# The first block of an FP4 feed-forward stage: a third pair of accumulators, products in fixed turn, an earlier table load, other PSUM banks

## The chip, the cores and the metric

The kernel runs on one core of a Trainium2 chip. The metric is the device time of one launch in microseconds. The engines named are TensorE (PE, its weight loads PEld), VectorE (DVE), ScalarE (ACT), GpSimd (POOL) and SyncE (SP, which here issues transfers).

## The reference

Two transformer layers run on 2 sequences of 1024 tokens with 512 channels. The change lies in the feed-forward part of the first layer, whose weights are stored as 4-bit numbers with a scale for every 128 inputs:

```python
def _L0_ffn_ref(x, gate_up_packed, gate_up_scales, down_packed, down_scales):
    I = gate_up_packed.shape[0] // 2                      # 1408
    w_gu = _dequant_fp4(gate_up_packed, gate_up_scales, 128)
    w_down = _dequant_fp4(down_packed, down_scales, 128)
    gate_up = einsum('bsh,oh->bso', x, w_gu)
    gate, up = gate_up[..., :I], gate_up[..., I:]
    h = silu(gate) * up
    y = einsum('bsi,hi->bsh', h, w_down)
    return y / sqrt(mean(y * y, -1) + 1e-6)

x = layernorm(x + L0_attn(x))      # stage 1 of the kernel
x = layernorm(x + L0_ffn(x))       # stage 2, the FP4 stage
x = layernorm(x + L1_attn(x))      # gated linear attention
x = layernorm(x + L1_ffn(x))       # routed feed-forward, top 512 of 1024 tokens
```

## The kernel before

The 2048 tokens are cut into four blocks of 512 (`NB = 4`), and the 512 channels into four slices of 128 (`KC = 4`), which are also the groups that share a scale. The 1408 hidden units are eleven tiles of 128 (`NI = 11`), numbered by `f`.

**Stage 1** is the linear attention of the first layer. For its last tiles it turns the queries (`transposed`, L197), multiplies them with a matrix (`project`, L217, tile `ao`), adds the result to the row of x on VectorE (L383) and takes statistics. Exponentials run on ScalarE (L270), and the queries are weighed on VectorE with a small tile `z` of two buffers (L355 to L360). At its end the FP4 scales are turned and copied (L399 to L403). The first block of x is split into a high and a low part, `x1Th` and `x1Tl`, which together stand for float32 in a faster format; their product with the unpacked weights `wgu` is two matmuls.

**Stage 2** runs over the blocks, and in each block over f. For one f, `scaled_sums` makes eight groups of two matmuls: for each of the four slices k a group for gate and one for up. A group fills one PSUM bank. For k = 0 ScalarE copies the bank, times its scale, into an accumulator (L470). For other k VectorE multiplies and adds into it (L476). For some f (`by_three`: odd f and f from 8 on in block 0) the last group of up goes another way: ScalarE copies it (L473) and GpSimd adds it (L474). Then ScalarE applies silu to gate (L660), and GpSimd multiplies with up into h (L661).

Accumulators are two "rooms" each for gate and up, taken in turn: f can begin to accumulate when h of f - 2 is made. PSUM has eight banks, given out in rings. Stage 2 splits them into a ring of six for gate and up (and the transposes) and a ring of two for the down products (L631). The bank of a group is fixed in the order of the program, so each group waits until the group six places before it has been read.

The order in which an engine gets its instructions comes from a scheduler, which follows the order of the program but may move an instruction that seems ready before others. `tc.issue_after(ins)` keeps all instructions of a `with` that are on the engine of `ins` behind `ins`. In the kernel before, the matmuls of each f stand behind the last one of the f before (L658); inside an f the groups are free. In f = 8 and 9 a function `quarter` puts in four transposes after k = 1 and after k = 3, which prepare the next block (`split_quarter`, L208 to L212).

In block 0, GpSimd also normalises the fourth block of x, a quarter after each of f = 0, 2, 4 and 6 (`norm_tiles`, L564 to L573, with one power L570). From the second block on, the down products of the block before (`down`, matmuls L512 and L521, tile `P`) follow the gate and up products of f = 1, 4 and 7; they use seven products of half size in place of eight, for which GpSimd makes sums of h (`S`, L527) and, in block 1, of the weights (`T1`, `T2`, `T4`, L457).

Of the kernel before, what the change touches and what calls it, by code (L numbers as in the profile page):

```python
# [10 lines left out]
F32 = mybir.dt.float32  # L11
# [4 lines left out]
AF = mybir.ActivationFunctionType  # L16
# [5 lines left out]
P = 128  # L22
# [4 lines left out]
NI = I_FF // P  # L27
# [46 lines left out]
def body(ctx: ExitStack, tc: tile.TileContext, a: dict, out: bass.AP):  # L74
    nc = tc.nc
# [5 lines left out]
    sp = ctx.enter_context(tc.tile_pool(name="small", bufs=3))  # L81
# [4 lines left out]
    rings, turn_of = {"mm": range(4), "acc": range(4, 8)}, {"mm": 0, "acc": 0}  # L86
# [6 lines left out]
    def mm_bank(name):  # L93
        return bank("mm", name)

    def acc_bank(name):
        return bank("acc", name)
# [4 lines left out]
    def const(name):  # L102
        at, n = _AT[name]
        return table[:, at : at + n]

    ident = const("ident")

    def place_w(i, name):
        return wpool.tile([P, KC, C], F32, tag=f"A{i}", name=name)
# [6 lines left out]
    def load_w(dst, name):  # L116
        nc.sync.dma_start(out=dst, in_=a[name].rearrange("(k p) o -> p k o", p=P))
# [73 lines left out]
    last_turned = [None]  # L191

    def transposed(x, name):

        pt = mm_bank(name)
        for k in range(KC):
            ins = nc.tensor.transpose(pt[:, k * P : (k + 1) * P], x[:, k * P : (k + 1) * P], ident).ins  # L197
        last_turned[0] = ins
        return pt

    def split_tiles(blk):

        i, j = ((1, 1), (2, 0), (0, 2), (1, 1))[blk]
        hi = xT_slot(i, "x1Th", F32R)
        lo = wpool.tile([P, KC, 512], F32R, tag=f"A{j}", name="x1Tl")
        return hi, lo

    def split_quarter(parts, blk, i):  # L208
        hi, lo = (t[:, :, i * P : (i + 1) * P] for t in parts)
        pt = transposed(x_t[blk][:, i], "x1Tp").rearrange("p (k t) -> p k t", k=KC)  # L210
        nc.scalar.copy(hi, pt)
        nc.vector.tensor_sub(lo, pt, hi.bitcast(F32))  # L212
# [9 lines left out]
    wgu = wfp4.tile([P, KC, 2 * I_FF], F32R, name="wgu")  # L222
# [56 lines left out]
    for b in range(B):  # L279
        acc = [acc_bank(f"xk{b}_{c}") for c in range(KC)]  # L280
# [18 lines left out]
        if b == 0:  # L299
            first = [mm_bank("kp") for _ in range(4)]  # L300
# [68 lines left out]
        for n in range(10):  # L369
# [5 lines left out]
            if n >= 1 and n <= 8:  # L375
                i = n - 1
                blk = 2 * b + i // 4
# [4 lines left out]
                x = x_t[blk][:, i % 4]  # L382
# [9 lines left out]
            if b == 1 and n in (2, 3, 4, 5):  # L392
                if n == 2:
                    parts = split_tiles(0)
# [6 lines left out]
    pg = mm_bank("pg")  # L401
    nc.tensor.transpose(pg[:, : KC * FG], sg, ident[: KC * FG, : KC * FG])
    nc.scalar.copy(scale, pg[:, : KC * FG])  # L403
    s1.close()


# [8 lines left out]
    def xT_tile(name):  # L415
        return xT_slot(next(free), name)

    def turn(blk, part=range(4)):

        if 0 in part:  # L420
            xT[blk] = xT_tile("x2T")
        for i in part:
            pt = transposed(x_t[blk][:, i], "x2Tp")
            nc.scalar.copy(xT[blk][:, :, i * P : (i + 1) * P], pt.rearrange("p (k t) -> p k t", k=KC))
        return last_turned[0]
# [14 lines left out]

    with tc.tile_pool(name="s2", bufs=1) as wk2:
        NP = (NI - 1) // 2
        rooms = {n: [wk2.tile([P, 512], F32, name=f"{n}{i}") for i in range(2)] for n in ("gate", "up")}
        spare, junk = b2, rw
        extra = [wk2.tile([P, 3, 512], F32, name="h_even")]
        T1, T2, T4 = (wk2.tile([P, NP, 256], F32, name=f"T{i}") for i in (1, 2, 4))
        S = wk2.tile([P, NP, 2, P], F32, name="S")
        extra.append(wk2.tile([P, 3, 512], F32, name="h_odd"))


# [3 lines left out]
        def sums_of_wdn():  # L454
            for dst, x, y in ((T1, B12, B11), (T2, B22, T1), (T4, B21, T2), (B12, B22, B12)):
                for j in (slice(0, 3), slice(3, NP)):
                    yield nc.gpsimd.tensor_sub(dst[:, j], x[:, j], y[:, j])  # L457

        def scaled_sums(f, parts, gate, up, by_three, beside=None):

            for k in range(KC):
                for acc, at, name in ((gate, f, "gatep"), (up, NI + f, "upp")):
                    ps = mm_bank(name)
                    for x in parts:
                        ins = nc.tensor.matmul(  # L465
                            ps, wgu[:, k, at * P : (at + 1) * P], x[:, k], start=x is parts[0], stop=x is parts[1]
                        ).ins
                    s = scale[:, k * FG + at : k * FG + at + 1]
                    if k == 0:
                        nc.scalar.activation(acc, ps, AF.Copy, scale=s)  # L470
                    elif k == KC - 1 and acc is up and by_three:
                        third = (spare, junk)[f % 2]
                        nc.scalar.activation(third, ps, AF.Copy, scale=s)  # L473
                        nc.gpsimd.tensor_add(acc, acc, third)  # L474
                    else:
                        last = nc.vector.scalar_tensor_tensor(acc, ps, s, acc, ALU.mult, ALU.add).ins  # L476
                if beside is not None:
                    beside(k)
            return ins, last

        class Hidden:
# [15 lines left out]

        of_S = lambda j: S[:, j]
        last_p = [None]
# [59 lines left out]
        def take(pieces, n):  # L559
            for _ in range(n):  # L560
                next(pieces, None)
# [66 lines left out]
                    yield  # L628
                layernorm(x_t[self.blk], self.mv)

        rings["mm"], rings["acc"] = (0, 1, 2, 3, 6, 7), (4, 5)  # L631
        wsums = sums_of_wdn()
        now, pieces = None, iter(())
        for blk in range(NB):
            h = Hidden(blk)
            for f in range(NI):
                if f == 0 and blk:
                    with tc.issue_after(hm):
                        take(pieces, 1)
                gate, up = (rooms[n][(blk * NI + f) % 2] for n in ("gate", "up"))  # L640
                if f == 8:

                    if blk < NB - 1:
                        coming = split_tiles(blk + 1)
                    else:
                        Wig = place_w(0, "Wig")
                        load_w(Wig, "WigT")

                def quarter(k):
                    if k % 2 and f in (8, 9):  # L650
                        i = 2 * (f - 8) + k // 2
                        if blk < NB - 1:
                            split_quarter(coming, blk + 1, i)
                        else:
                            turn(0, (i,))

                by_three = f % 2 == 1 or f >= 8 if blk == 0 else f >= 8 and blk < NB - 1
                with tc.issue_after(mm) if blk or f else ExitStack():  # L658
                    mm, st = scaled_sums(f, parts, gate, up, by_three, quarter)
                sl = nc.scalar.activation(gate, gate, AF.Silu).ins  # L660
                hm = nc.gpsimd.tensor_mul(h.chunk(f), up, gate).ins  # L661
                with tc.issue_after(mm), tc.issue_after(st), tc.issue_after(hm), tc.issue_after(sl):
                    if blk == 0 and f in (0, 2, 4, 6):
                        norm_tiles(3, late, (f // 2,))
                    for _ in range((1, 5, 1, 1)[f] if blk == 1 and f < 4 else 0):
                        next(wsums)
                    if blk > 1 and f in old_steps:
                        old_steps[f]()

                    if blk and f in (1, 4, 7):  # L670
                        take(pieces, {1: 22, 4: 32, 7: 24}[f])
                        mm = last_p[0]
                    if blk == NB - 1 and f == 9:
                        now.squares(range(4))
                        now.power()
            parts = coming
            old, now = now, Normed(blk)
            pieces = down(h, now.room)
            if blk > 0:
                old_steps = old.steps()  # L680
# [52 lines left out]
    T1, T2, T4 = gsums[1][:, 1], gsums[2][:, 0], gsums[2][:, 1]  # L733
# [44 lines left out]
    def scores(blk, gates, beside=None):  # L778
# [51 lines left out]
        for i in range(4):  # L830
# [4 lines left out]
            nc.tensor.matmul(up, gates.kd[:, t].rearrange("p r d -> p (r d)"), x_t[blk][:, i], start=True, stop=True)  # L835
            S = wk.tile([P, C], F32, tag="S", name="S", bufs=4)
            if t == 0:
                ins = nc.vector.tensor_copy(S, up).ins
            else:
                ins = nc.vector.scalar_tensor_tensor(  # L840
                    S, state[blk // 2, t], decay[:, i : i + 1], up, ALU.mult, ALU.add
                ).ins
            state[blk // 2, t + 1] = S
        return ins

    def attend(blk):
# [4 lines left out]
        for c in range(KC):  # L851
            op = mm_bank("op")
            cut = slice(c * P, (c + 1) * P)
            for i in range(4):
                S = state.get((blk // 2, 4 * (blk % 2) + i))
                oi = op[:, i * P : (i + 1) * P]
# [557 lines left out]
```

## Time and profile before

| what | us |
|---|---|
| median of 3 runs | 1013.36 (1012.85 to 1015.86) |
| profiled execution, its own time | 1015.42 |
| its span, first to last instruction | 1013.6 |
| TensorE busy | 990.1 (98%) |
| VectorE busy | 645.6 (64%) |
| GpSimd busy | 299.5 (30%) |
| ScalarE busy | 276.1 (27%) |
| first unhoisted gate product of block 0 | at 253.65 |
| first down product (block 1, after f = 1) | at 313.83 |
| end of the FP4 stage's last product (about) | at 552.8 |

Times inside the span are counted from its first instruction. A busy time says how long an engine worked and not whether anything waited for it; whether a wait matters is read from the timeline of the engine that sets the pace in that stretch.

### The profile page before, as it was taken

How to read it: one execution, taken by the hardware profiler on the slowest of the kernel's cores; microseconds unless marked ns; L12 is line 12 of the kernel's file. 1: busy time of each engine (PE TensorE's matmuls, PEld its weight loads, DVE VectorE, ACT ScalarE, POOL GpSimd, SP SyncE). 2: the span in 40 equal slices, each digit the busy share in tenths (PEclk: the TensorE clock that was granted, in tenths of full speed). 3: DMA queues.
4: the chain of work that ended last, by engine and by line, in shares of the span. 5: the costliest groups of instructions: out<-in, count | busy, mean ns of one | idle time of the engine just before them, and what ended most of it. 6: DMA issues, size and time to landing. Idle time of an engine off the chain costs nothing.

```text
span 1013.6 us, 10955 instructions
## 1 busy us (share of the span) xinstructions
PE 990.1 (98%) x4061; PEld 709.1 (70%) x4061; DVE 645.6 (64%) x1233; ACT 276.1 (27%) x465; POOL 299.5 (30%) x277
## 2 busy tenths in 40 slices
PE   8999999999899999999999999999999999999996
PEld 3454444544668888888888854687777688888885
DVE  1246754476786576676666258556698795789744
ACT  2223232232453235235233143142130124220000
POOL 1100351004567626566556103201014003000022
PEclk9999999999999999999999999999999999999999
DMA  9611113110000000000011140000003412140011
GB/s 345 199 52 57 43 58 113 32 32 0 1 1 0 1 1 1 1 1 11 1 42 42 40 179 0 1 1 0 1 7 108 126 52 84 42 167 1 0 42 42
DMA packets 25688, 48.81 MB, mean 48 GB/s; under 512 B 4652, under 2 KB 6316, under 8 KB 25123
## 3 DMA queue, kind: packets, MB, share of 16 engines
q1 hardware_dynamic: 22995, 42.85, 12.8%
q0 software_dynamic: 1920, 4.22, 1.1%
q10 hardware_dynamic: 720, 1.05, 0.3%
q8 instruction: 32, 0.52, 0.2%
q14 instruction: 21, 0.17, 0.1%
HBM read 39.70 MB, written 10.52 MB: 50 GB/s over the span
## 4 chain that ended last, share of the span: by engine, by line
PE 83%; issue 8%; DVE 4%; ACT 2%; POOL 2%; DMA 0%; POOLq 0%; ACTq 0%; DVEq 0%
PE P L512 12%; PE yp L1158 9%; PE hp L1079 9%; PE gatep L465 8%; PE upp L465 8%; PE qp L217 5%; PE xk L286 5%; PE ao L217 5%; PE kp L217 4%; PE ao L962 3%; PE go L918 2%; PE kp L303 1%; PE lp L432 1%; PE P L521 1%; PE up L835 1%
## 5 line engine op out<-in xcount | busy, mean ns | idle before, releaser
L181 POOL TENSOR_TENSOR rs<-rs,table 128x4 f32<-128x4 f32 (+1 forms) x21 | 19.6, 937 | 324.4 <-DVE rs L180 324.1
L476 DVE SCALAR_TENSOR_TENSOR gate<-gatep,scale,gate 128x512 f32<-128x512 f32 x132 | 98.1, 743 | 13.9 <-PE gatep L465 8.7
L476 DVE SCALAR_TENSOR_TENSOR up<-upp,scale,up 128x512 f32<-128x512 f32 x119 | 88.4, 743 | 2.5 <-PE upp L465 1.5
L465 PE MATMUL gatep<-x1Th,wgu 128*128 128x512 f32 x176 | 73.7, 428 | 4.0 <-ACT gate L470 3.5
L465 PE MATMUL upp<-x1Th,wgu 128*128 128x512 f32 x176 | 70.0, 402 | 0.4 <-ACT gate L470 0.4
L465 PE MATMUL upp<-x1Tl,wgu 128*128 128x512 f32 x176 | 69.1, 396 | 0.0
L465 PE MATMUL gatep<-x1Tl,wgu 128*128 128x512 f32 x176 | 68.5, 398 | 0.0
L661 POOL TENSOR_TENSOR h<-up,gate 128x512 f32<-128x512 f32 x32 | 41.1, 1285 | 85.7 <-ACT gate L660 80.6
L470 ACT ACTIVATE gate<-gatep,scale 128x512 f32<-128x512 f32 x44 | 30.3, 689 | 123.7 <-PE gatep L465 106.7
L512 PE MATMUL P<-wdn,h 128*128 128x256 f32 x256 | 60.5, 379 | 0.0
L217 PE MATMUL qp<-Wq,x0T 128*128 128x512 f32 x128 | 57.6, 592 | 0.0
L217 PE MATMUL ao<-G,qT 128*128 128x512 f32 x128 | 57.5, 595 | 0.0
L286 PE MATMUL xk<-k,x 128*128 128x512 f32 x128 | 56.7, 592 | 0.0
L962 PE MATMUL ao<-W1o,uT 128*128 128x512 f32 x128 | 55.6, 592 | 0.0
L512 PEld LDWEIGHTS P<-wdn,h 128*128 128x128 f32 x256 | 48.5, 190 | 6.8
L866 POOL TENSOR_TENSOR sum<-sum,sq 128x512 f32<-128x512 f32 x12 | 18.2, 1518 | 107.6 <-issue 83.7
L286 PEld LDWEIGHTS xk<-k,x 128*128 128x128 f32 x128 | 24.3, 190 | 30.6 <-issue 29.9
L217 PEld LDWEIGHTS ao<-G,qT 128*128 128x128 f32 x128 | 24.1, 190 | 30.2 <-issue 28.9
L271 DVE SCALAR_TENSOR_TENSOR k<-kp,e 128x512 f32<-128x512 f32 x16 | 11.0, 691 | 53.7 <-ACT e L270 48.2
L465 PEld LDWEIGHTS gatep<-x1Th,wgu 128*128 128x128 f32 x176 | 32.9, 190 | 16.9 <-ACT gate L470 9.6
L962 PEld LDWEIGHTS ao<-W1o,uT 128*128 128x128 f32 x128 | 24.0, 190 | 28.7 <-issue 27.7
L217 PE MATMUL kp<-Wk,x0T 128*128 128x512 f32 x96 | 43.4, 593 | 0.2 <-DVE k L271 0.2
(338 smaller groups left out, 2125.7 us busy)
## 6 DMA issues: line engine op xcount, KB each, us to landing
pk<-in_gu SPq DMA_DIRECT2D x16, 352.0 KB, 3.8
x<-in_x SPq DMA_DIRECT2D x4, 1024.0 KB, 12.8
w<-in_w SPq DMA_DIRECT2D x1, 4096.0 KB, 14.7
xs<-picked SPq DMA_DIRECT2D x4, 1024.0 KB, 5.1
out<-x SPq DMA_DIRECT2D x4, 1024.0 KB, 4.5
w<-in_w SPq DMA_DIRECT2D x4, 1024.0 KB, 6.6
x0T<-in_xT SPq DMA_DIRECT2D x3, 1024.0 KB, 8.8
pk<-in_dn SPq DMA_DIRECT2D x11, 256.0 KB, 3.5
```

The source lines that it names most:

```text
L181: power = nc.gpsimd.tensor_tensor(rs[:, :n], rs[:, :n], const("mhalf")[:, :n], ALU.pow).ins
L217: nc.tensor.matmul(ps, lhs[:, k], w[:, k], start=start and k == 0, stop=stop and k == KC - 1)
L286: nc.tensor.matmul(acc[c], x_t[2 * b + i // 4][:, i % 4, c * P : (c + 1) * P], k, start=i == 0, stop=i == 7)
L465: ins = nc.tensor.matmul(ps, wgu[:, k, at * P : (at + 1) * P], x[:, k], start=x is parts[0], stop=x is parts[1]).ins
L470: nc.scalar.activation(acc, ps, AF.Copy, scale=s)
L476: last = nc.vector.scalar_tensor_tensor(acc, ps, s, acc, ALU.mult, ALU.add).ins
L512: last_p[0] = nc.tensor.matmul(cut, x(j)[:, r], w[:, j], start=j == 0, stop=j == NP - 1 and tail is None).ins
L661: hm = nc.gpsimd.tensor_mul(h.chunk(f), up, gate).ins
L918: nc.tensor.matmul(ps[:, 256 * m : 256 * m + 256], w[:, k, m], b[:, k, 256 * half : 256 * half + 256], start=k == 0, stop=k == KC - 1,)
L962: nc.tensor.matmul(ao[i], uT[blk][:, k, i * P : (i + 1) * P], W1o[:, k], start=n == 0, stop=n == 3)
L1079: nc.tensor.matmul(ps[:, 256 * j : 256 * j + 256], w[:, k, 2 * g + j], x[:, k], start=k == 0, stop=k == 1)
L1158: nc.tensor.matmul(ps[:, 256 * r : 256 * r + 256], x(r, j), w(j), start=j == 0, stop=j == NJ - 1)
```

## The change

Four things change. Block 0 has three rooms for gate and up, the third lying in the tile `T4`, which is not written until block 1; later blocks keep two. Inside an f each group of matmuls stands behind the group before it in program order, and so do the transposes of `quarter`. A one-column silu at the end of stage 1, which writes a `z` buffer that nothing reads, puts silu's table load there. The down products get the two banks that stage 1's last accumulations used, here 6 and 7, and gate and up get the other six.

```diff
+    nc.scalar.activation(sp.tile([P, 16], F32, tag="z", name="first", bufs=2)[:, :1], ident[:, :1], AF.Silu)
     s1.close()
...
-        rooms = {n: [wk2.tile([P, 512], F32, name=f"{n}{i}") for i in range(2)] for n in ("gate", "up")}
+        rooms = [[wk2.tile([P, 512], F32, name=f"{n}{i}") for n in ("gate", "up")] for i in range(2)]
...
         S = wk2.tile([P, NP, 2, P], F32, name="S")
+
+        rooms.append([T4.rearrange("p j c -> p (j c)")[:, i * 512 : (i + 1) * 512] for i in range(2)])
...
         def scaled_sums(f, parts, gate, up, by_three, beside=None):
+            ins = None
             for k in range(KC):
                 for acc, at, name in ((gate, f, "gatep"), (up, NI + f, "upp")):
                     ps = mm_bank(name)
-                    for x in parts:
-                        ins = nc.tensor.matmul(
-                            ps, wgu[:, k, at * P : (at + 1) * P], x[:, k], start=x is parts[0], stop=x is parts[1]
-                        ).ins
+                    with ExitStack() if ins is None else tc.issue_after(ins):
+                        for x in parts:
+                            ins = nc.tensor.matmul(
+                                ps, wgu[:, k, at * P : (at + 1) * P], x[:, k], start=x is parts[0], stop=x is parts[1]
+                            ).ins
...
-                if beside is not None:
-                    beside(k)
+                with tc.issue_after(ins):
+                    ins = beside(k) or ins
             return ins, last
...
-        rings["mm"], rings["acc"] = (0, 1, 2, 3, 6, 7), (4, 5)
+        rings["acc"] = [4 + (turn_of["acc"] + i) % 4 for i in (2, 3)]
+        rings["mm"] = [i for i in range(8) if i not in rings["acc"]]
...
-                gate, up = (rooms[n][(blk * NI + f) % 2] for n in ("gate", "up"))
+                gate, up = rooms[f % 3 if blk == 0 else (f + blk - 1) % 2]
...
                             turn(0, (i,))
+                        return last_turned[0]
```

## The prediction

> **What bounds the kernel now.** I read the page first: TensorE is busy 98% of the span, and the chain of waits that ended last is 83% TensorE. A change gains only where TensorE has holes. The windows by stage tell where they are. Columns: window, length, then the busy time of PE, PEld, DVE, ACT and POOL with counts, granted clock, DMA share, GB/s.
>
> ```profile
> 269.00:277.00 8.00, 7.53 (x25) 5.75 (x26) 4.74 (x7) 4.10 (x7) 5.24 (x4) 0.79 0.00 0
> ...
> 253.65:313.83 60.18, 55.44 (x226) 40.51 (x224) 49.81 (x76) 31.39 (x50) 35.87 (x29) 0.97 0.00 1
> ...
> 314.00:552.80 238.80, 238.80 (x1093) 199.69 (x1093) 161.50 (x255) 84.45 (x152) 139.31 (x135) 1.00 0.04 11
> ```
>
> Blocks 1 to 3 of the FP4 stage (314 to 552.8) have no idle time on TensorE. The first block, with two f of the second (253.65 to 313.83, where the down products begin), has 4.7 us of it, and a clock of 0.79 in one stretch. The waits of TensorE in that window (waiter, releaser, us in total, times, longest) name ScalarE's first scaled copy of a group:
>
> ```profile
> PE gatep L465 <- ACT gate L470: 3.5, 5, 2.2
> ...
> PE upp L465 <- ACT gate L470: 0.4, 1, 0.4
> ```
>
> Next the timelines (start, length, engine, line, operation, idle time before and its releaser). TensorE:
>
> ```profile
> 266.61 0.39 PE L465 MATMUL gatep<-x1Th,wgu 128*128 128x512 f32 x1
> 266.84 0.40 PE L465 MATMUL gatep<-x1Tl,wgu 128*128 128x512 f32 x1
> 269.47 0.80 PE L465 MATMUL gatep<-x1Th,wgu 128*128 128x512 f32 x1 [2.23 <-ACT gate L470]
> 270.06 0.63 PE L465 MATMUL gatep<-x1Tl,wgu 128*128 128x512 f32 x1
> 270.49 0.63 PE L465 MATMUL upp<-x1Th,wgu 128*128 128x512 f32 x1
> 270.91 0.63 PE L465 MATMUL upp<-x1Tl,wgu 128*128 128x512 f32 x1
> ```
>
> A fed TensorE starts a product every 0.2335 us (266.61, 266.84). After the hole of 2.23 us the starts lie 0.425 us apart until 272.62. ScalarE and GpSimd show why:
>
> ```profile
> 259.62 1.28 ACT L660 ACT_TABLE_LOAD   x1
> 260.91 0.64 ACT L660 ACTIVATE gate<-gate 128x512 f32<-128x512 f32 x1
> ...
> 268.73 0.69 ACT L470 ACTIVATE gate<-gatep,scale 128x512 f32<-128x512 f32 x1 [3.98 <-POOL h L661]
> ```
>
> ```profile
> 261.63 1.30 POOL L661 TENSOR_TENSOR h<-up,gate 128x512 f32<-128x512 f32 x1 [14.81 <-ACT gate L660]
> 262.88 1.03 POOL L570 TENSOR_TENSOR rs<-rs,table 128x4 f32<-128x4 f32 x1
> 264.02 2.08 POOL L573 TENSOR_SCALAR x<-x,mv,rs 128x512 f32<-128x512 f32 x1
> 266.06 1.29 POOL L474 TENSOR_TENSOR up<-up,rw 128x512 f32<-128x512 f32 x1
> 267.43 1.26 POOL L661 TENSOR_TENSOR h<-up,gate 128x512 f32<-128x512 f32 x1
> ```
>
> The copy of f = 3 (268.73) writes the room that f = 1 used; that room is free when GpSimd has made h of f = 1 (267.43 + 1.26). GpSimd is late because silu of f = 0 waited for its table (259.62), then came the power, a norm and the addition to up. While ScalarE waits, its bank stays full, and TensorE runs out of banks six groups on.
>
> **The working of the loss.** From 253.65 to 313.83 TensorE issues 207 gate and up products (176 of block 0, less one hoisted to 246.70, and 32 of f = 0 and 1 of block 1) and 16 transposes (0.09 each, from four in 0.36): 207 x 0.2335 + 16 x 0.09 = 48.3 + 1.4 = 49.8 us. The window is 60.2, so 10.4 are lost. By start-to-start times: the hole of 266.84 and the slow products after it, 4.1; five holes before which an f has its k = 0 copies late (263.15, 277.94, 282.90, 286.81, 291.78), about 3.0 with their restarts; holes round the transposes (295.43, 300.91, 303.12), 2.0; the start, 0.5; small restarts of 0.1, 0.8. The four near 0.54 are not the room alone: the copy waits there for its product ("ACT gate L470 <- PE gatep L465: 12.0, 9, 2.2" in the same waits), since inside an f the products run out of turn. At 277.24 gate's k = 0 comes as one of the last of its f, and the group six banks on needs its bank at once.
>
> [...] the trace has 1.28 and silu at once after it, so I use 1.28. [...] the trace has copies after the exponentials and after silu with no further load.
>
> **The change part by part.** *Table.* One load of 1.28 leaves the path 259.62 to 260.91, and a load plus a one-column activation appear in stage 1. No row shows that small one; the nearest is the 128x88 copy, 0.24 us (L403), and it can't be under 0. Both lie beside other work: ScalarE idles from 247.65 to 254.84, and from 242.9 to 246.44, while TensorE runs ao. The small tile takes a z buffer, free after L360 of tile 6 (241.32), which is after the last exponential (238.60), so no second load follows. Cost 0; were the cover gone (ahead of a qT copy), up to 1.5. Everything of f = 0 on ScalarE and GpSimd is 1.3 earlier.
>
> *Rooms.* f waits for h of f - 3 instead of f - 2. By the rows: h of f = 0 is done near 261.7, norm near 265, up's addition of f = 1 near 266.2, its h near 267.5, h of f = 2 near 269.2, h of f = 3 near 273.8. The copies want them at 266.1 (f = 3, of 261.7), 269.9 (f = 4, of 267.5), 273.6 (f = 5, of 269.2), 277.3 (f = 6, of 273.8). None waits. What is late next is VectorE. T4 as third room costs nothing: its own sums on GpSimd come in block 1, behind h of f = 8 on the same engine. Later blocks keep two rooms at the same distance.
>
> *Order.* k = 0 goes first in each f, so its bank has six groups (2.8 us) to come free; the copy needs 0.66 from the last product's start and 0.69. TensorE's new waits hold all products behind them, where before another group could step in. Transposes now stand after group k = 1 and 3, as blocks 1 and 2 already run them with 0.08 lost each.
>
> *Banks.* Ring position 5 was bank 7, last read by the addition at 254.25; the trace has 0.28 of weight-load wait for it at 254.99. The new pair left to the down products is 6 and 7, needed only 50 us later. Gain 0.1, within the start's 0.5.
>
> **The sum.** TensorE alone gives 49.8. VectorE is the other floor: 59 accumulations of block 0 (11 x 6 less 7 taken by ScalarE and GpSimd), 12 of block 1 and 4 subtractions, 0.66 apart in this pair:
>
> ```profile
> 257.24 0.74 DVE L476 SCALAR_TENSOR_TENSOR gate<-gatep,scale,gate 128x512 f32<-128x512 f32 x1
> 257.90 0.74 DVE L476 SCALAR_TENSOR_TENSOR up<-upp,scale,up 128x512 f32<-128x512 f32 x1
> ```
>
> 75 x 0.66 = 49.5 from 255.85 gives 305.4; TensorE's last product can start 1.3 ahead of that end, so down products start at 304.3 at the earliest, against 303.5 by TensorE. I keep 2.0 lost (start 0.5, joints of transposes 0.4, restarts and VectorE's jitter 1.1): 60.2 - 49.8 - 2.0 = 8.4 gained. In blocks 1 to 3 eight pairs of small restarts, 0.18 each, could go with the order (up to 1.4), or new waits arise; no row shows which, I take 0. After 314 TensorE sets the pace, and its other waits (scan, router, last scatter) follow it, so 8.4 reach the end. Span 1013.6 - 8.4 = 1005.2; the profiled execution took 1015.4 (1.8 round the span), so 1007.0. The median before is 1013.36, 2.1 below that execution; I put the difference on the median: **1005.0 us**.
>
> **Rivals.** *VectorE becomes the bound.* For it: 75 starts against a PE need of the same size, so every VectorE hole counts. With 4 us of its 10 us of holes left, 8.4 falls to 4.4: 1009.0. Against: six banks buffer 2.8 us.
>
> *The change doesn't do what it says: only the table matters.* If the schedule on GpSimd or ScalarE reforms the waits, the big hole shrinks by 1.3 and the slow clock with it goes (1.4): 2.7 gained, 1010.7; with the clock still slow, 1012, no change.
>
> *Strict turns cost more than they give* (slower). In blocks 1 to 3 two rooms remain, and TensorE may no longer step past a full bank. It decides where h of f - 2 ends more than 2.3 us (five groups) after the product k = 0 of f. In block 1, h of f = 2 ends at 330.95 and that product starts at 330.79, so 2 us are spare. A loss of 0.4 in each of 33 f is 13.2, less 8.4: 1018.2. The zero idle of those blocks speaks against it.
>
> **Numbers.** About 0.3% (3 us) is what a measurement here can tell from no change. Main case 0.63, VectorE 0.20, table only 0.11 (half of it within 3 us), strict turns 0.06. Faster 0.63 + 0.20 + 0.05 = 0.88, same 0.07, slower 0.05. Low end: all 10.4 and half of the 1.4, 1002.3. High end: into the table case, 1010.3.
>
> **What would show it.** Right: no table load at L660, one in stage 1 before 254; no wait of GpSimd's h in front of L470 in block 0; clock 1.00 throughout 253 to 305; gate and up alternating; first down product near 305.4; blocks 1 to 3 still without idle. Wrong: a wait of TensorE on L470 or L476 of over 1 us in block 0, down products after 309, or idle TensorE between block 1 and 3.

## The result and the profile after

The changed kernel takes 1004.17 us (median of 4 runs, 1003.83 to 1005.26), the kernel before, run beside it, 1014.61. The ratio is 0.990, with a 95% interval of 0.9879 to 0.9921, or 8 to 12 us less. The forecast was 1005.0, in a range of 1002.3 to 1010.3. The times of the kernel before lie in two groups, about 1013.4 and about 1015.8 (what sets them apart is told below), and the profile of it that is shown is of the upper group.

The span is 1002.0 against 1013.6. The windows of the changed kernel (columns as in those of before):

```profile
253.65:304.00 50.35, 50.35 (x226) 40.61 (x226) 49.45 (x77) 28.68 (x49) 36.56 (x29) 1.00 0.00 1
304.00:541.00 237.00, 237.00 (x1090) 199.07 (x1089) 160.00 (x254) 84.30 (x152) 138.75 (x134) 1.00 0.03 11
```

In the first block TensorE has no idle time left, at full clock, and VectorE is busy for 49.45 of 50.35 us. The whole program's waits of TensorE (waiter, releaser, us in total, times, longest) name neither L471 (the gate and up products, L465 before) nor L518 (the down products, L512 before). The longest three are in other stages and are those of before, to the tenth:

```profile
PE kp L303 <- DMA x0T<-in_xT: 4.6, 1, 4.6
PE dp L828 <- DVE last L813: 1.5, 2, 1.2
PE ep L781 <- ACT l L770: 1.3, 1, 1.3
```

ScalarE's timeline at the end of stage 1 has the table:

```profile
241.90 1.28 ACT L405 ACT_TABLE_LOAD   x1
243.19 0.20 ACT L405 ACTIVATE first<-table 128x1 f32<-128x1 f32 x1
245.40 1.08 ACT L365 COPY qT<-qTp 128x512 f32<-128x512 f32 x2 [2.01 <-PE qTp L197]
```

The load and the small activation end 2.01 us before the next copy, which still waits for TensorE. GpSimd's timeline shows what answers to the row that was late before:

```profile
263.71 1.30 POOL L480 TENSOR_TENSOR up<-up,rw 128x512 f32<-128x512 f32 x1
265.08 1.30 POOL L671 TENSOR_TENSOR h<-up,gate 128x512 f32<-128x512 f32 x1
266.81 1.30 POOL L671 TENSOR_TENSOR h<-T 128x512 f32<-128x512 f32 x1 [0.43 <-ACT T L670]
268.09 2.08 POOL L579 TENSOR_SCALAR x<-x,mv,rs 128x512 f32<-128x512 f32 x1
```

Here h of f = 1 ends at 266.38, while ScalarE makes silu of f = 2 in the third room (`T`). ScalarE's copy of f = 3 began at 264.94 already; it waited for its own product and not for this h:

```profile
264.94 0.69 ACT L476 ACTIVATE gate<-gatep,scale 128x512 f32<-128x512 f32 x1 [1.90 <-PE gatep L471]
```

The down products begin at 303.30:

```profile
303.07 0.39 PE L471 MATMUL upp<-x1Tl,wgu 128*128 128x512 f32 x1
303.30 1.89 PE L518 MATMUL P<-wdn,h 128*128 128x256 f32 x8
```

The span of each profile falls into four stretches, read from the first and last start of `ao`, `P` and `lp`:

| stretch | before | after | gain |
|---|---|---|---|
| start to last product of attention (`ao`) | 253.6 | 252.6 | 1.0 |
| to the first down product (`P`) | 60.2 | 50.7 | 9.5 |
| to the first product of the next layer's logits (`lp`) | 239.0 | 237.9 | 1.1 |
| to the end | 460.9 | 460.9 | 0 |

The 1.0 of the first stretch isn't the change's: the last product of the first keys starts between 19.6 and 20.9 in the profiles of this study, in no order with the edits (what goes with it is told under the two times of the kernel before). The change gave 9.5 in the block that it is about and 1.1 in blocks 1 to 3. Of the 9.5, 1.3 are slow products that only the upper group of the kernel before has.

### The profile page after: what moved, and what is told of

The parts are those of the page before. It is cut to its first block, busy times and chain, and to the rows that moved or that the text cites. A ratio compares the mean times of both kernels' runs of the same rounds, so it can differ in the third digit from the quotient of the medians.

```text
span 1002.0 us, 10997 instructions
## 1 busy us (share of the span) xinstructions
PE 983.1 (98%) x4061; PEld 708.8 (71%) x4061; DVE 644.6 (64%) x1233; ACT 274.7 (27%) x466; POOL 299.2 (30%) x277
## 4 chain that ended last, share of the span: by engine, by line
PE 84%; issue 8%; DVE 4%; POOL 2%; ACT 1%; DMA 0%; POOLq 0%; DVEq 0%; ACTq 0%
PE P L518 12%; PE yp L1168 9%; PE hp L1089 9%; PE upp L471 8%; PE gatep L471 8%; PE qp L217 5%; PE xk L286 5%; PE ao L217 5%; PE kp L217 4%; PE ao L972 3%; PE go L928 2%; PE lp L434 1%; PE kp L303 1%; PE P L527 1%; PE up L845 1%
## 5 line engine op out<-in xcount | busy, mean ns | idle before, releaser
L181 POOL TENSOR_TENSOR rs<-rs,table 128x4 f32<-128x4 f32 (+1 forms) x21 | 19.6, 936 | 324.2 <-DVE rs L180 323.9
L482 DVE SCALAR_TENSOR_TENSOR gate<-gatep,scale,gate 128x512 f32<-128x512 f32 x123 | 91.3, 742 | 7.3 <-PE gatep L471 6.7
L482 DVE SCALAR_TENSOR_TENSOR up<-upp,scale,up 128x512 f32<-128x512 f32 x112 | 83.0, 741 | 0.2
L471 PE MATMUL gatep<-x1Th,wgu 128*128 128x512 f32 x176 | 73.0, 415 | 0.0
L471 PE MATMUL upp<-x1Th,wgu 128*128 128x512 f32 x176 | 69.8, 397 | 0.0
L471 PE MATMUL gatep<-x1Tl,wgu 128*128 128x512 f32 x176 | 69.6, 395 | 0.0
L471 PE MATMUL upp<-x1Tl,wgu 128*128 128x512 f32 x176 | 69.5, 395 | 0.0
L671 POOL TENSOR_TENSOR h<-up,gate 128x512 f32<-128x512 f32 x30 | 38.6, 1286 | 78.3 <-ACT gate L670 73.3
L518 PE MATMUL P<-wdn,h 128*128 128x256 f32 x256 | 60.5, 379 | 0.0
L217 PE MATMUL ao<-G,qT 128*128 128x512 f32 x128 | 57.5, 594 | 0.2 <-ACT qT L365 0.2
L518 PEld LDWEIGHTS P<-wdn,h 128*128 128x128 f32 x256 | 48.5, 190 | 6.7
L188 DVE BATCH_NORM_STATS2 st<-x 128x6 f32<-128x512 f32 x64 | 42.8, 682 | 0.8
```

The source lines that it names most:

```text
L188: nc.vector.bn_stats(st, x)
L217: nc.tensor.matmul(ps, lhs[:, k], w[:, k], start=start and k == 0, stop=stop and k == KC - 1)
L471: ins = nc.tensor.matmul(ps, wgu[:, k, at * P : (at + 1) * P], x[:, k], start=x is parts[0], stop=x is parts[1]).ins
L518: last_p[0] = nc.tensor.matmul(cut, x(j)[:, r], w[:, j], start=j == 0, stop=j == NP - 1 and tail is None).ins
```

## The experiments

The theory was that each part removes its own term of the 10.4 us lost in block 0: rooms and table the hole at f = 3, the turn the late k = 0 products and the holes round the transposes. Its rivals were that one part does everything (the table, or the rooms), that strict turns cost, and that VectorE takes over as the bound. Four kernels have one part of the change alone, four lack one part.

**One part alone.** The table:

```diff
+    nc.scalar.activation(sp.tile([P, 16], F32, tag="z", name="first", bufs=2)[:, :1], ident[:, :1], AF.Silu)
```

> Silu's table loaded in stage 1, nothing else changed. My theory (each part removes its own term of the 10.4 us lost in block 0, and turn and rooms carry most): the hole at f = 3 shrinks by the 1.28 us of the load to about 1, and the slow products after it (1.4) may go; the holes at the other f and round the transposes stay: 1.3 to 2.7 us faster, about 1012. Rival (the late table starts the whole row of stalls): over 7 us faster, 1007 or less.

Three rooms:

```diff
+        rooms.append([T4.rearrange("p j c -> p (j c)")[:, i * 512 : (i + 1) * 512] for i in range(2)])
...
-                gate, up = (rooms[n][(blk * NI + f) % 2] for n in ("gate", "up"))
+                gate, up = rooms[f % 3 if blk == 0 else (f + blk - 1) % 2]
```

> Three rooms in block 0, nothing else changed: groups inside an f still free, table and banks as before. My theory: the hole at f = 3 and its slow products (4.1) go, the late k = 0 products inside each f (3.0) and the holes at the transposes (2.0) stay: 3.5 to 5 us faster, about 1010, first down product near 309.5. Rival (the rooms are all): 8 us or more faster, 1006. Second rival (rooms do nothing while the k = 0 products come late): within 1.5 us.

Groups in turn:

```diff
+                    with ExitStack() if ins is None else tc.issue_after(ins):
...
+                with tc.issue_after(ins):
+                    ins = beside(k) or ins
...
+                        return last_turned[0]
```

> Groups strictly in turn, with two rooms, table and banks as before. My theory: the late k = 0 products and the holes round the transposes go (5 us together), the small restarts of blocks 1 to 3 go (1.1 us, as the changed kernel shows), but the wait for h of f - 2 stays and is now waited for in turn, so part of the 5 comes back: 2 to 6 us faster, about 1010. Rival (strict turns without the third room stall TensorE more than they free it): 1 us or more slower than before, over 1015. Second rival (the turn is all): 8 us or more faster.

The banks:

```diff
-        rings["mm"], rings["acc"] = (0, 1, 2, 3, 6, 7), (4, 5)
+        rings["acc"] = [4 + (turn_of["acc"] + i) % 4 for i in (2, 3)]
+        rings["mm"] = [i for i in range(8) if i not in rings["acc"]]
```

> Only the banks of the two rings are exchanged. My theory: the wait of 0.28 us for the addition at 254.25 goes and nothing else: within 0.5 us of the kernel before. Rival (a new ring order shifts the holes): 1.5 us or more either way.

**One part taken back.** The same edits, each undone in the changed kernel, the other three kept.

> The changed kernel without the early silu: the table is loaded in front of silu of f = 0 again. My theory: with three rooms and turns the 1.28 us are taken up by the slack of the rooms (h of f = 1 would end near 267.7, the third room lets f = 3 begin without it): 0 to 1 us slower than the changed kernel, about 1004.5. Rival (ScalarE's copies of f = 1 and 2 queue behind the load and hold banks): 1.3 to 3 us slower, about 1006.

> The changed kernel with two rooms in block 0. My theory: waits for h of f - 2 on GpSimd come back where a norm stands between (f = 3, 5, 7), 1 to 2 us each at the most: 3 to 5 us slower than the changed kernel, about 1008. Rival (with the table early and the turn kept, two rooms suffice): within 1 us of the changed kernel.

> The changed kernel with the groups inside an f free again. My theory: k = 0 products come late inside an f again, and transposes break in: 4 to 6 us slower than the changed kernel (3.0 and 2.0 of block 0, 1.1 of blocks 1 to 3), about 1009. Rival (the products ran out of turn only because the rooms were taken): within 1.5 us of the changed kernel.

> The changed kernel with the rings' banks as before. My theory: the third group of block 0 waits for the addition of the last attention tile, about 0.3 us, and nothing can step in front of it now, so the whole row of products begins later: 0.2 to 0.9 us slower than the changed kernel. Rival (the wait repeats round the ring): 1.5 us or more slower.

Measured (ratio to runs of the kernel before taken beside it, with its 95% interval; the two stretches from one profile each, `ao` to `P` and `P` to `lp`). The ratio weighs both groups of the kernel before, so it differs a little from the quotient of the medians: the turn alone is 6.6 us faster by its ratio and 5.8 by the medians.

| kernel | median us | ratio | ao to P | P to lp |
|---|---|---|---|---|
| before (32 runs beside the first four) | 1013.84 | 1 | 60.2 | 239.0 |
| table alone | 1012.26 | 0.9978 (0.9970 to 0.9986) | 57.5 | 239.0 |
| rooms alone | 1011.77 | 0.9973 (0.9964 to 0.9982) | 56.6 | 239.0 |
| turn alone | 1008.05 | 0.9935 (0.9922 to 0.9949) | 54.0 | 237.7 |
| banks alone | 1013.79 | 0.9997 (0.9987 to 1.0006) | 60.2 | 239.0 |
| all but the table | 1004.30 | 0.9895 (0.9879 to 0.9910) | 50.8 | 237.8 |
| all but the rooms | 1006.47 | 0.9915 (0.9901 to 0.9928) | 52.4 | 237.9 |
| all but the turn | 1011.45 | 0.9965 (0.9952 to 0.9979) | 56.2 | 238.9 |
| all but the banks | 1004.78 | 0.9900 (0.9885 to 0.9915) | 50.9 | 237.8 |
| all (the changed kernel) | 1004.17 | 0.9900 (0.9879 to 0.9921) | 50.7 | 237.9 |

*The turn is the largest part*: 6.6 us alone by its ratio, and 7 lost where it is missing. In the trace of turn alone none of the holes of 0.54 is left, neither inside an f nor round the transposes; the two halves of the edit (the groups, the transposes) were not run apart. It is also the only part that moves blocks 1 to 3: every kernel with it has 237.7 to 237.9 there, every kernel without it 238.9 or 239.0. The eight pairs of small restarts, 0.18 each, that the prediction saw there are in the trace of rooms alone and gone in that of turn alone. The timeline of rooms alone shows that a third room doesn't cure the order. TensorE first, then ScalarE:

```profile
272.70 0.39 PE L467 MATMUL gatep<-x1Th,wgu 128*128 128x512 f32 x1
272.93 0.40 PE L467 MATMUL gatep<-x1Tl,wgu 128*128 128x512 f32 x1
273.17 0.39 PE L467 MATMUL upp<-x1Th,wgu 128*128 128x512 f32 x1
273.40 0.40 PE L467 MATMUL upp<-x1Tl,wgu 128*128 128x512 f32 x1
274.17 0.73 PE L467 MATMUL gatep<-x1Th,wgu 128*128 128x512 f32 x2 [0.37 <-ACT T L472]
```

```profile
273.43 0.69 ACT L472 ACTIVATE T<-gatep,scale 128x512 f32<-128x512 f32 x1 [1.67 <-PE gatep L467]
274.01 0.68 ACT L472 ACTIVATE T<-upp,scale 128x512 f32<-128x512 f32 x1
```

The third room is free and ScalarE has idled 1.67 us for the product of k = 0, which ran as one of the last of its f. The copy begins at 273.43, and the group that needs this bank waits for its end (274.12; it starts at 274.17). The hole of 0.54 (274.17 - 273.40 - 0.23) is the same as before; four of them and those round the transposes are in the traces of rooms alone and of all but the turn.

*The rooms* gave less than expected: 2.7 by the ratio against 3.5 to 5, though the stretch `ao` to `P` is 3.6 shorter. The hole at f = 3 is gone, as expected. The 3.6 are counted from the profile before, which is of the upper group; about half of the runs before lack its slow products (see below), and from their stretch of 58.9 it is 2.3. With the turn in place their lack costs 2.2 (1006.47 against 1004.30 of all but the table, run beside it), against 3 to 5 expected, and no wait of TensorE is listed in that stretch at all. The waits for h came back where they were expected, on ScalarE, before the copies of f = 3, 5 and 7 (3.37, 2.92 and 2.91 us), but they cost TensorE less. ScalarE at f = 3, then TensorE:

```profile
267.44 0.69 ACT L475 ACTIVATE gate<-gatep,scale 128x512 f32<-128x512 f32 x1 [3.37 <-POOL h L670]
268.03 0.68 ACT L475 ACTIVATE up<-upp,scale 128x512 f32<-128x512 f32 x1
```

```profile
267.57 0.39 PE L470 MATMUL upp<-x1Th,wgu 128*128 128x512 f32 x1
267.81 0.40 PE L470 MATMUL upp<-x1Tl,wgu 128*128 128x512 f32 x1
268.18 0.49 PE L470 MATMUL gatep<-x1Th,wgu 128*128 128x512 f32 x1
268.51 0.39 PE L470 MATMUL gatep<-x1Tl,wgu 128*128 128x512 f32 x1
268.76 0.50 PE L470 MATMUL upp<-x1Th,wgu 128*128 128x512 f32 x1
```

Products start 0.37 and 0.33 us apart in place of 0.2335, because each group finds its bank only just read: the copies end at 268.13 and 268.71, the groups that follow in their banks start at 268.18 and 268.76. Sixteen such restarts of about 0.1 us are 1.6 of the 1.7 us by which this stretch exceeds that of the changed kernel. Here the six banks, filled in turn, take up most of a wait of 3.37 us on ScalarE.

*Turn with neither rooms nor early table* (turn alone) has one true hole, at f = 3, of 1.0 us in place of 2.2, and restarts elsewhere. So strict turns did not cost more than they gave; that rival falls.

*The table* is worth 2.2 alone and nothing that can be measured once rooms and turn are there: all but the table loads it at 259.44, in front of silu of f = 0, and still has a median of 1004.30. The table-only rival falls, and the early load is redundant beside the other two parts; which of them makes it so was not run apart.

*The banks* give nothing that can be told from no change: 0.9997 alone, and undone a median 0.5 above that of all but the table, beside it, with 50.9 from `ao` to `P` against 50.8. In the traces one late start of 0.1 us, at 254.99 in the profile before, goes with the exchange of the banks; that is the 0.1 of the prediction.

**Is VectorE the next floor?** In the changed kernel four more accumulations go to VectorE:

```diff
-                by_three = f % 2 == 1 or f >= 8 if blk == 0 else f >= 8 and blk < NB - 1
+                by_three = f >= 8 and blk < NB - 1
```

> The changed kernel, but in block 0 the last group of up goes by ScalarE and GpSimd only for f of 8 and more, so that VectorE gets 4 accumulations more. My theory (VectorE is the floor just under TensorE): 4 x 0.66 = 2.6 us more on VectorE, of which about 0.5 finds idle time; the first down product comes 1.5 to 2.5 us later than in the changed kernel and the whole is 1.5 to 2.5 slower, about 1006. Rival (six banks and the down products hide it, or GpSimd's relief pays): within 0.5 us of the changed kernel.

Measured 1006.14 (1005.63 to 1007.14), 2.0 over the changed kernel, which ran at another time (1003.83 to 1005.26), and 52.4 from `ao` to `P` against 50.7. Its window:

```profile
253.50:306.00 52.50, 52.50 (x228) 40.01 (x227) 52.06 (x82) 26.57 (x45) 31.72 (x25) 1.00 0.00 1
```

VectorE is busy for 52.06 of 52.5 us, and TensorE loses its time in restarts of 0.1, two at each f. VectorE stood less than 1 us below TensorE in this block, and with 2.6 more it is the bound.

**Why the kernel before has two times.** Its 32 runs beside the first four kernels lie in two groups, 17 from 1012.9 to 1013.9 and 15 from 1015.4 to 1016.1. It was profiled twice more, unchanged:

> The kernel before, unchanged: its timed executions lie in two groups, near 1013.3 and near 1015.9, and the profile shown is one of the upper. My theory: in the upper group the hole at f = 3 is followed by products at half rate, in the lower it isn't, so an execution near 1013 shows a last attention product to first down product of about 58.8 instead of 60.2 and a clock of 1.00 there. Rival: the groups differ at the start of the program (the first keys end at 19.6 to 20.9 in the runs so far) and that stretch is 60.2 in both.

> As for before_look1: a second look at the kernel before, to meet the other group.

They took 1013.11 and 1013.95, both of the lower group, both with 58.9 from `ao` to `P`. TensorE in the first:

```profile
265.89 0.40 PE L465 MATMUL gatep<-x1Tl,wgu 128*128 128x512 f32 x1
268.53 0.50 PE L465 MATMUL gatep<-x1Th,wgu 128*128 128x512 f32 x1 [2.25 <-ACT gate L470]
268.87 0.40 PE L465 MATMUL gatep<-x1Tl,wgu 128*128 128x512 f32 x1
269.10 0.39 PE L465 MATMUL upp<-x1Th,wgu 128*128 128x512 f32 x1
269.33 0.40 PE L465 MATMUL upp<-x1Tl,wgu 128*128 128x512 f32 x1
```

The same hole (2.25 us) is followed here by products at the full rate, 0.23 apart, where the upper group has 0.425.

The granted clock goes with the rate of the products. In the profile before it is 0.50 from 269.25 to 272.60, and 1.00 both from 268 to 269.2, in the hole, and from 272.65 to 274, when the products run at the full rate again. The four profiles that have the hole of 2.2 us:

| profile | hole, us | mean granted clock, in the window |
|---|---|---|
| before | 2.23 | 0.86, 263 to 275 |
| banks alone | 2.2 | 0.86, 263 to 275 |
| before, first further profile | 2.25 | 1.00, 266 to 274 |
| before, second further profile | 2.25 | 1.00, 266 to 274 |

The holes are alike to 0.1 us, so their length doesn't tell the two kinds apart, and what does isn't shown.

The start of the program differs too. In the profile before, the products of the first keys start 0.85 us apart up to 9.03, and 0.43 apart from 9.85 on; in the changed kernel's the first spacing ends at 7.33 and the second begins at 7.96, and the last of these products starts at 19.55 in place of 20.58. In the first further profile it starts at 19.6. The spans of that profile and of the one before differ by 2.3 us: 1.3 are the slow products and about 1.0 the later start. The two groups of times lie 2.5 apart. So both the theory and its rival hold a part, but a late start alone doesn't put an execution into the upper group: the second further profile has one (20.5) and took 1013.95. What sets the moment at which the spacing changes isn't shown.

## Why the prediction was right

*The place and the bound* hold: all of the gain lies between 253 and 541, the stage that follows is unchanged to a tenth, and no idle time is left in the FP4 stage.

*Rooms.* The times worked out for h of f = 0 to 3 (261.7, 267.5, 269.2, 273.8) are met: in the changed trace they end at 260.56, 266.38, 268.11 and 272.80, each about 1.1 earlier, as that profile's whole stage is 1.0 earlier. No copy waits for them.

*Table.* It went where the prediction put it, behind tile 6's z and ahead of the last qT copies, at 1.28 + 0.20 us and no cost; the small activation starts 0.01 us after the load's end.

*The sum* had 8.4 and the profiles show 10.6 (9.5 + 1.1). Four terms were off. The residue was set at 2.0 and is 0.7 (0.4 at the start, and 0.09 at each of four joints of products and transposes): the 1.1 for restarts and VectorE's jitter did not come. The block has 208 products in place of 207, since the gate product that ran at 246.70 before stays in its turn now: 0.2 less gained. Blocks 1 to 3 were taken at 0 of up to 1.4 and gave 1.1, all of it by the turn. And 1.4 of slow products were counted as gained, while the median that the gain was taken from, 1013.36, belongs to the group without them. From that median the fall is 9.2, which is 8.4 + 1.3 - 0.2 + 1.1 - 1.4. The mechanism held; that the forecast came within 1 us of the time is luck, since terms that were off cancelled.

*The VectorE floor* was right in size, wrong in its rule. The prediction let TensorE's last product start at most 1.3 us ahead of VectorE's end. In the changed trace VectorE's last accumulation of that row starts at 304.76 and ends at 305.5, and TensorE's last product starts at 303.07, 2.4 ahead: six banks let it lead by several groups, not by one latency. So the down products followed TensorE's own floor: 303.5 predicted, 304.3 measured with this profile's 1.0 put back, and the 0.7 of residue with the one product more account for the difference. That 304.3 is also the VectorE floor of the prediction is chance: no wait and no restart beyond those 0.7 is left to VectorE. The rival with VectorE as the bound did not come about, by less than 1 us of VectorE's time (49.45 of 50.35 us busy).

*The shares* were the weakest step. "Five holes" of 3.0 and "holes round the transposes" of 2.0 add up to 5.0 for the turn; with 1.1 in the later blocks that is 6.1, and it measured 6.6 alone and 7 when undone. The hole at f = 3 with its slow products, 4.1 in the sum (3.9 by the starts: 266.84 to 272.62 for eight products), measured 2.7 by the rooms alone and 2.2 when they were undone, since the turn, the table and the rooms each relieve it. The four single gains (2.2, 2.7, 6.6 and 0.3) make 11.8, the change 10; each of the first three contains the slow products, which can go only once.

## What to carry to other kernels

When a ring of buffers is assigned in program order but instructions may run in another, a late first group is waited for by the group one ring length on; look for an evacuation that waits for its own product right before a hole. More buffers don't cure that; a fixed order does, and the two together are worth less than their sum. After such a repair count the next engine's starts over the same stretch: here it stood 1 us below. And when the times of one kernel fall into two groups, take the gain and the time that it is taken from out of the same group; the forecast here mixed them.

## What the runs showed of the hardware

A hole of 2.2 us on TensorE was followed by a lower granted clock in two of four profiled executions (mean 0.86 from 263 to 275) and by the full clock in the other two (1.00 from 266 to 274); three are of the kernel before, one has the banks exchanged. In the profile before, the clock was 0.50 from 269.25 to 272.60, with 0.425 us between starts of products, against 0.2335 at 1.00. After holes of 1.28 us (table alone) and 1.0 us (turn alone) the granted clock stayed at 1.00 up to the first down product.

Products of float32 operands (the first keys, 128x512) started 0.43 us apart from 9.85 us on in the profile before; those of the split rows (fp32r, L465, also 128x512) started 0.2335 apart.

In all but the rooms, products that found their bank only just read, with no wait listed, started about 0.1 us late; sixteen of these cost 1.6 us, with TensorE shown busy for 52.40 of 52.40 us.
